# A mirrored, paired layout of attention factors: two long runs for one matmul, two runs for another

## The chip, the cores and the metric

The kernel runs on one core of a Trainium2 chip. The metric is the device time of one execution in microseconds (us), as the median of several runs; less is better. The inputs are 16 graphs of 1024 nodes with 256 features, in fp32, and a 1024 x 1024 int32 adjacency matrix for each.

## The reference, cut to what matters

Each graph goes through two layers, each followed by a residual and a layer norm. The first weighs neighbours by a sigmoid of a leaky-ReLU score. The second is a graph attention layer with 4 heads of 64 features:

```
Wh    = (X @ W).reshape(B, N, H, F)
e     = leaky_relu(e_src[:, :, None, :] + e_dst[:, None, :, :], 0.2)
e     = where(A > 0, e, -1e9)
alpha = softmax(e, axis=2)
Hout  = elu(einsum('bijh,bjhf->bihf', alpha, Wh))
```

The exponential of a leaky ReLU of a sum is exp(s+d) where s+d >= 0 and exp(0.2(s+d)) elsewhere; both split into a factor of the row i and a factor of the column j. So the layer needs, for each row and head, the sum of exp(d_j) Wh_j over the edges with s+d >= 0, and the sum of exp(0.2 d_j) Wh_j over the other edges. The kernel gets the latter as the sum over all edges less the sum over the positive ones.

## The kernel before, in words

Every graph is worked in blocks of 128 nodes (P = 128; NB = 8 blocks; NH = 2 halves of 512 rows; H = 4 heads; F = 64; E = 2F + 2 = 130 columns of factors for each head; F1 = F + 2 = 66).

- **Factors.** `exps` (L598 to L601, ScalarE) makes es[1] = exp(d), es[0] = exp(0.2 d) and rho = exp(-0.8 s). `product` (L619, VectorE) multiplies them into Wh, head by head. `high` (L633, ScalarE) rounds each product to fp32r into the tile `gm`, and `low` (L640, VectorE) puts the remainder of the rounding beside it. `gm` is one tile for the whole run, shaped [128, head, block, level, 130]: level 0 the rounded part, level 1 the remainder. The 130 columns are 64 of exp(d) Wh, 64 of exp(0.2 d) Wh, and the two exponentials.
- **Sums over positive edges.** `pos` (L658, VectorE) makes for a half, a head and a block the 0/1 matrix of positive edges [128 x 512]. `acc` (L670, TensorE) takes it in four slices of 128 as weights, and streams the two levels of one head and block, 260 columns in a row. There are 256 such matmuls for a graph. `acc_low` (L685, ScalarE) copies the low half out of PSUM and `acc_sum` (L693, VectorE) adds the halves into the tile `u`.
- **Sums over all edges.** `all_edges` (L705) casts the mask to fp32r; `total` (L713, TensorE) streams, for each block and level, the columns 64 to 130 of all four heads: four runs of 66 columns, 264 in all. There are 128 such matmuls for a graph. `total_kept` (L749) and `total_less` (L755) take the result out of PSUM.
- **The end of a graph.** `weigh` (L772, L780), `divide` (L790 to L795), `elu` (L816) and `join` (L807, L810) combine the parts in `u`, and the norm follows. In the last graph the fourth head of the second half has steps of its own (`weigh_end` L826, `divide_end` L837 to L848, `elu_end` L855, `join_end` L865, L867). The last two graphs scale on ScalarE (L767) in the function `times`.
- **The other TensorE work** is the score matmuls of the first layer (L356), its aggregation (L427), the projection (L517) and transposes (L319, L395, L498).

The order of all work on every engine is written out by hand: each step of each stage has a due time in a table (TIMES for the middle graphs, FIRST and LAST for the first and the last), a graph's times are shifted by PERIOD = 112, and `issue` calls the steps in the order of these times. So the stages of two or three graphs are interleaved. Semaphore waits follow from which tiles, or which parts of a tile, an instruction touches.

Of the kernel before, what the change touches and what calls it, by code (L numbers as in the profile page):

```python
# [8 lines left out]
F32 = mybir.dt.float32  # L9
F32R = mybir.dt.float32r  # L10
# [3 lines left out]
I32 = mybir.dt.int32  # L14
AF = mybir.ActivationFunctionType
ALU = mybir.AluOpType
# [3 lines left out]
SLOPE = 0.2  # L20
# [7 lines left out]
P = 128  # L28
HALF = 512
# [164 lines left out]
def stages(nc, k, pl, b, xg, adjg, outg, sums, span, zinv):  # L194


    H, F, D, N, NB, DC, NH = k.H, k.F, k.D, k.N, k.NB, k.DC, k.NH
    F1, WD, E = k.F1, k.WD, k.E
    NQ = NB // NH
    HEADS = [(half, h) for half in range(NH) for h in range(H)]  # L200

    TOTALS = [*range(NQ, NB), *range(NQ)]

    first, last, late = b == 0, b == k.B - 1, b >= k.B - 2
    t = {}

    def bank(name):
# [5 lines left out]
    def small(name, *shape, bufs=None):  # L213
        return pl.small.tile([P, *shape], F32, tag=name, name=name, bufs=bufs)
# [43 lines left out]
    def aload():  # L258
        for ib in range(NB):
            if first and 2 <= ib < 6:  # L260

                tile = pl.us.tile([P, 2, H, E], F32, tag="us", name="a_us")
                tile = tile.rearrange("p q h e -> p (q h e)")[:, 0:N].bitcast(I32)
            else:
                tile = pl.adjp.tile([P, N], I32, tag="a32", name="a32")
            t["a32", ib] = tile
            nc.sync.dma_start(out=t["a32", ib], in_=adjg[ib * P : (ib + 1) * P, :])
            yield
# [325 lines left out]
        yield  # L594

    def exps():
        es = t["es"] = small("es", 2, NB, H)
        nc.scalar.activation(es[:, 1], t["cm"], AF.Exp)  # L598
        nc.scalar.activation(es[:, 0], t["cm"], AF.Exp, scale=SLOPE)
        t["rho"] = small("rho", NB, H)  # L600
        nc.scalar.activation(t["rho"], t["sd"], AF.Exp, scale=SLOPE - 1.0)  # L601
        yield


    FACTORS = [(h, s) for h in range(H) for s in range(2)]

    def product():
        for h, s in FACTORS:
# [15 lines left out]

    def factor(h, s):
        if s == 0:
            yield slice(2 * F, E), t["es"][:, :, :, h].rearrange("p s b -> p b s")
        yield slice(s * F, (s + 1) * F), t["prod", h, s]

    def high():  # L630
        for h, s in FACTORS:
            for cols, val in factor(h, s):
                nc.scalar.copy(pl.gm[:, h, :, 0, cols], val)  # L633
            yield

    def low():
        for h, s in FACTORS:
            for cols, val in factor(h, s):
                hi = pl.gm[:, h, :, 0, cols].bitcast(F32)
                nc.vector.tensor_tensor(pl.gm[:, h, :, 1, cols], val, hi, ALU.subtract)  # L640
            yield


# [20 lines left out]
    def acc():  # L664
        for half, h in HEADS:
            for pair in range(NQ // 2):
                t["acc", half, h, pair] = pl.ps_u.tile([P, 2, HALF], F32, tag="u", name="acc")
            for jb in range(NB):
                for q in range(NQ):
                    nc.tensor.matmul(  # L670
                        t["acc", half, h, q // 2][:, q % 2, 0 : 2 * E],
                        lhsT=t["pos", half, h, jb][:, q * P : (q + 1) * P],
                        rhs=pl.gm[:, h, jb].rearrange("p l f -> p (l f)"),
                        start=(jb == 0),
                        stop=(jb == NB - 1),
                    )
                yield
# [10 lines left out]
    def acc_sum():  # L688
        for half, h in HEADS:
            for pair in range(NQ // 2):  # L690
                if h == 0:
                    t["u", half, pair] = pl.us.tile([P, 2, H, E], F32, tag="us", name="u")
                nc.vector.tensor_tensor(  # L693
                    t["u", half, pair][:, :, h, :],
                    t["acc", half, h, pair][:, :, 0:E],
                    t["low", half, h, pair], ALU.add,
                )
                yield


    def all_edges():
# [6 lines left out]
    def total():  # L708
        for ib in TOTALS:
            tot = t["tot", ib] = bank("tot")  # L710
            for jb in range(NB):
                for l in range(2):
                    nc.tensor.matmul(  # L713
                        tot[:, 0 : H * F1],
                        lhsT=t["allm", ib, jb // 4 * 4][:, jb % 4, :],
                        rhs=pl.gm[:, :, jb, l, F:E],
                        start=(jb == 0 and l == 0),
                        stop=(jb == NB - 1 and l == 1),
                    )
                if jb % 2:  # L720
                    yield

    def heads_of(tot):
        return tot[:, 0 : H * F1].rearrange("p (h f) -> p h f", h=H)

    def heads(half):

        return slice(0, H - 1 if last and half else H)

    def parts(half, pair, hs):  # L730

        u = t["u", half, pair][:, :, hs]
        return u[..., 0:F], u[..., F : 2 * F], u[..., 2 * F], u[..., 2 * F + 1]

    def second(half, pair):

        return t["u", half, pair][..., F : 2 * F + 1]

    def nodes(half, pair):
        return t["y", half][:, 2 * pair : 2 * pair + 2, :].rearrange(  # L740
            "p q (h f) -> p q h f", h=H
        )

    def total_kept():
        for ib in TOTALS[:NQ]:
            pair, q = divmod(ib - NQ, 2)
            if q == 0:
                t["ts", pair] = pl.ts.tile([P, 2, H, F1], F32, tag="ts", name="ts")
            nc.scalar.copy(t["ts", pair][:, q], heads_of(t["tot", ib]))  # L749
            yield  # L750

    def total_less():
        for ib in TOTALS[NQ:]:
            u = second(0, ib // 2)[:, ib % 2]
            nc.vector.tensor_tensor(u, heads_of(t["tot", ib])[..., 0 : F + 1], u, ALU.subtract)  # L755
            yield

    PAIRS = [(half, pair) for half in range(NH) for pair in range(NQ // 2)]  # L760

    def times(val, by):

        if late:
            for q in range(2):
                for h in range(val.shape[2]):
                    nc.scalar.activation(  # L767
                        val[:, q, h, :], val[:, q, h, :], AF.Copy, scale=by[:, q, h : h + 1]
                    )
        else:  # L770
            by = by.unsqueeze(3).to_broadcast(list(val.shape))
            nc.vector.tensor_tensor(val, val, by, ALU.mult)  # L772

    def weigh():
        for half, pair in PAIRS:
            ib, hs = half * NQ + 2 * pair, heads(half)
            u2 = second(half, pair)[:, :, hs]
            if half:
                ts = t["ts", pair][:, :, hs, 0 : F + 1]
                nc.vector.tensor_tensor(u2, ts, u2, ALU.subtract)  # L780
                yield
            times(u2, t["rho"][:, ib : ib + 2, hs])
            yield

    def divide():
        t["rz"] = small("rzs", NB, H)
        for half, pair in PAIRS:
            ib, hs = half * NQ + 2 * pair, heads(half)
            o, u2, z2, z1 = parts(half, pair, hs)
            nc.vector.tensor_tensor(o, o, u2, ALU.add)  # L790
            yield
            rz = t["rz"][:, ib : ib + 2, hs]
            nc.vector.scalar_tensor_tensor(rz, z1, Z_MIN, z2, ALU.max, ALU.add)
            yield
            nc.vector.reciprocal(rz, rz)  # L795
            yield
            times(o, rz)
            yield


    def join():
        for half, pair in PAIRS:
            o, ex, _, _ = parts(half, pair, heads(half))
            yp = nodes(half, pair)[:, :, heads(half)]
            rows = (0, 1) if last and half else (slice(0, 2),)
            for q in rows:
                nc.vector.scalar_tensor_tensor(o[:, q], o[:, q], 0.0, yp[:, q], ALU.max, ALU.add)  # L807
            yield
            for q in rows:
                nc.vector.scalar_tensor_tensor(yp[:, q], ex[:, q], 1.0, o[:, q], ALU.min, ALU.add)  # L810
            yield
# [10 lines left out]
    def weigh_end():  # L822
        for h, pair in END:
            if last:
                u2 = second(1, pair)[:, :, h]
                nc.vector.tensor_tensor(u2, t["ts", pair][:, :, h, 0 : F + 1], u2, ALU.subtract)  # L826
            yield

    def divide_end():
# [529 lines left out]
def gnn_resnorm_kernel(  # L1359
# [14 lines left out]
    nc = tc.nc  # L1374
    const = ctx.enter_context(tc.tile_pool(name="const", bufs=1))
    B, N, D = x.shape
    H = a_src.shape[0]
# [10 lines left out]
    with ExitStack() as fast:  # L1388
# [11 lines left out]
        with tc.tile_pool(name="first", bufs=1) as first:  # L1400
            make_constants(nc, k, const, first)
        pl.fill()
        pl.gm = pl.big.tile([P, H, NB, 2, k.E], F32R, tag="gm", name="gm")
        with tc.manual_schedule():
            issue(graphs)
        bad = pl.small.tile([P, 4], F32, tag="bad", name="bad", bufs=1)
# [71 lines left out]
```

## Time and profile before

| what | us |
|---|---|
| median of 3 runs (lowest, highest) | 1742.5 (1742.15, 1743.12) |
| span of the profiled execution | 1739.6 |
| what lies around that span, by the median of the runs | 2.9 |
| TensorE matmul busy | 1692.1 (97%) |
| VectorE busy | 1639.6 (94%) |
| ScalarE busy | 1239.4 (71%) |
| GpSimd busy | 106.8 (6%) |

The time of the profiled execution is not given beside its span, so the span stands for it and the 2.9 us are carried over from the runs. Busy time of TensorE counts a matmul from its first column to its drained result, so neighbours overlap: an `acc` matmul lasts 283 ns, but the next one starts far earlier. The chain view cuts that overlap: it follows the work that ended last back in time, and gives for each piece only the time that it added.

### The profile page before, as it was taken

The page shows a single profiled execution, that of the slowest core. Times are in us where ns is not written, and L with a number is a line of the kernel's source. Part 1 is how long each engine was busy: PE and PEld are TensorE (multiplying, and loading weights), DVE is VectorE, ACT ScalarE, POOL GpSimd, SP SyncE. Part 2 cuts the span into 40 slices and gives each one's busy share as a digit, 9 for nine tenths or more (in the row PEclk, how much of TensorE's full clock was granted, in tenths as well). Part 3 has the DMA queues.
Part 4 walks back from the last instruction along what each step waited for, and adds up shares of the span by engine and source line. Part 5 has one row for each costly group of instructions (what it writes and reads, how often), then busy time and mean ns, then how long its engine had stood idle before and what let it go on. Part 6 is the DMA issues. An engine that isn't in the chain of part 4 may idle for free.

```text
span 1739.6 us, 29647 instructions
## 1 busy us (share of the span) xinstructions
PE 1692.1 (97%) x10580; PEld 1492.5 (86%) x10580; DVE 1639.6 (94%) x3663; ACT 1239.4 (71%) x2766; POOL 106.8 (6%) x138
## 2 busy tenths in 40 slices
PE   8999999999999999999999999999999999999984
PEld 5789898998979889898998979889898898979883
DVE  5498999999999999999999999999999999999998
ACT  7674957759587685967759587685967859586784
POOL 0000000010000101000010000101000010000100
PEclk9999999999999999999999999999999999999987
DMA  5542333434334343333435334443343424422020
GB/s 190 129 116 67 98 98 92 110 92 131 88 89 101 105 125 92 94 101 92 109 92 129 91 86 102 105 128 91 89 107 92 110 67 117 105 71 55 26 68 26
DMA packets 249005, 168.59 MB, mean 97 GB/s; under 512 B 133010, under 2 KB 232468, under 8 KB 248852
## 3 DMA queue, kind: packets, MB, share of 16 engines
q1 hardware_dynamic: 248848, 166.63, 36.1%
q8 instruction: 86, 1.41, 0.3%
q14 instruction: 67, 0.55, 0.1%
q10 hardware_dynamic: 4, 0.00, 0.0%
HBM read 118.10 MB, written 17.04 MB: 78 GB/s over the span
## 4 chain that ended last, share of the span: by engine, by line
PE 91%; DVE 3%; ACT 2%; DMA 1%; issue 1%; POOL 0%; SPq 0%; ACTq 0%; DVEq 0%; POOLq 0%
PE acc L670 27%; PE agg L427 24%; PE tot L713 14%; PE e L356 13%; PE pw L517 7%; PE pg L395 3%; PE pt L498 2%; PE pt L319 1%; DVE pos L658 1%; DMA sbc<-sdram 1%; ACT prod L614 0%; DMA aT<-a 0%; PE pbc L591 0%; ACT gm L633 0%; ACT y L489 0%
## 5 line engine op out<-in xcount | busy, mean ns | idle before, releaser
L658 DVE SCALAR_TENSOR_TENSOR pos<-sbc,nd,mT 128x512 fp32r<-128x512 f32 x1024 | 737.4, 745 | 10.5 <-PE acc L670 5.0
L670 PE MATMUL acc<-gm,pos 128*128 128x260 f32 x4096 | 608.6, 292 | 8.9 <-DVE gm L640 5.0
L670 PEld LDWEIGHTS acc<-gm,pos 128*128 128x128 f32 x4096 | 536.8, 190 | 19.8 <-issue 5.7
L427 PE MATMUL agg<-xb,gate 128*128 128x256 f32 x2048 | 463.5, 379 | 0.2
L427 PEld LDWEIGHTS agg<-xb,gate 128*128 128x128 f32 x2048 | 379.9, 190 | 47.6 <-DVE gate L419 1.2
L713 PE MATMUL tot<-gm,allm 128*128 128x264 f32 x2048 | 328.8, 297 | 5.4 <-ACT gm L633 4.9
L713 PEld LDWEIGHTS tot<-gm,allm 128*128 128x128 f32 x2048 | 281.4, 189 | 9.7 <-ACT gm L633 5.1
L356 PE MATMUL e<-xT,xTa 128*128 128x512 f32 (+3 forms) x768 | 264.3, 489 | 2.2 <-ACT xTa L344 1.4
L356 PEld LDWEIGHTS e<-xT,xTa 128*128 128x128 f32 x768 | 135.1, 191 | 106.4 <-issue 55.3
L685 ACT COPY low<-acc 128x260 f32<-128x260 f32 x256 | 89.8, 377 | 187.5 <-PE acc L670 187.3
L705 ACT CAST allm<-mT 128x512 fp32r<-128x512 uint8 x256 | 157.4, 615 | 33.4 <-PE tot L713 31.7
L489 ACT ACTIVATE y<-y,shift,rstd 128x256 f32<-128x256 f32 x254 | 136.3, 592 | 48.6 <-DVE shift L477 48.6
L276 ACT ACTIVATE a<-a 128x1024 bf16<-128x1024 int32 x124 | 131.3, 1059 | 32.1 <-DMA aT<-a 23.0
L298 ACT ACTIVATE mT<-aT 128x1024 uint8<-128x1024 bf16 x120 | 127.1, 1059 | 7.6 <-DMA aT<-a 7.5
L468 POOL TENSOR_SCALAR std<-mv 128x4 f32<-128x4 f32 x64 | 27.7, 432 | 1618.7 <-DVE mv L450 1447.1
L517 PE MATMUL pw<-w_aug,yT 128*128 128x264 f32 x512 | 121.8, 387 | 0.5 <-ACT yT L507 0.5
L376 DVE TENSOR_TENSOR gate<-e,gate 128x512 f32<-128x512 f32 x192 | 105.5, 556 | 14.5 <-ACT gate L368 14.4
L693 DVE TENSOR_TENSOR u<-acc,low 128x260 f32<-128x260 f32 x256 | 103.1, 425 | 10.5 <-ACT low L685 10.3
L444 DVE BATCH_NORM_STATS2 st<-y 128x6 f32<-128x256 f32 x256 | 107.5, 421 | 1.2
L517 PEld LDWEIGHTS pw<-w_aug,yT 128*128 128x128 f32 x512 | 93.4, 190 | 15.4 <-ACT yT L507 1.9
L368 ACT ACTIVATE gate<-e 128x512 f32<-128x512 f32 x192 | 90.2, 486 | 13.7 <-PE e L356 13.3
L412 DVE TENSOR_TENSOR gate<-gate,mT 128x1024 f32<-128x1024 f32 (+7 forms) x128 | 96.6, 755 | 2.9 <-ACT mT L298 2.4
(111 smaller groups left out, 1788.8 us busy)
## 6 DMA issues: line engine op xcount, KB each, us to landing
a<-in_adj_dram SPq DMA_DIRECT2D x124, 512.0 KB, 4.6
sbc<-sdram SPq DMA_DIRECT2D x128, 256.0 KB, 4.6
out_dram<-y SPq DMA_DIRECT2D x31, 512.0 KB, 3.5
xb<-in_x_dram SPq DMA_DIRECT2D x15, 1024.0 KB, 5.4
a_us<-in_adj_dram SPq DMA_DIRECT2D x4, 512.0 KB, 8.9
aT<-a SPq DMA_TRANSPOSE x120, 3.1
xb<-in_x_dram SPq DMA_DIRECT2D x2, 512.0 KB, 4.7
sdram<-srow SPq DMA_DIRECT2D x32, 8.0 KB, 1.4
```

The costliest lines, as they stand in the source:

```text
L276: nc.scalar.activation(t["a16", ib], t["a32", ib], AF.Copy, accum_out=sums[:, 0, at : at + 1])
L298: nc.scalar.activation(t["mT"][:, :, ib * P : (ib + 1) * P], t["aT", ib], AF.Square, accum_out=sums[:, 1, at : at + 1],)
L356: nc.tensor.matmul(e[:, 0:n], lhsT=t["xTa", jb][:, c, :], rhs=t["xT"][:, c, at : at + n], start=(c == 0), stop=(c == DC - 1),)
L376: nc.vector.tensor_tensor(ge, t["e", jb, at][:, 0:n], ge, ALU.max)
L427: nc.tensor.matmul(agg[:, 0:D], lhsT=t["gate"][:, jb, ib * P : (ib + 1) * P], rhs=t["xb"][:, jb, :], start=(jb == 0), stop=(jb == NB - 1),)
L444: nc.vector.bn_stats(st, t["y", half][:, q, :])
L489: nc.scalar.activation(y, y, AF.Identity, bias=shift, scale=rstd)
L517: nc.tensor.matmul(pw[:, 0:WD], lhsT=t["yT"][:, c, jb * P : (jb + 1) * P], rhs=k.w_aug[:, c, :], start=(c == 0), stop=(c == DC - 1),)
L658: nc.vector.scalar_tensor_tensor(p_, t["sbc", half, h], t["nd"][:, jb, h : h + 1], t["mT"][:, jb, half * HALF : (half + 1) * HALF], ALU.is ...
L670: nc.tensor.matmul(t["acc", half, h, q // 2][:, q % 2, 0 : 2 * E], lhsT=t["pos", half, h, jb][:, q * P : (q + 1) * P], rhs=pl.gm[:, h, jb] ...
L705: nc.scalar.copy(m_, t["mT"][:, j0 : j0 + 4, ib * P : (ib + 1) * P])
L713: nc.tensor.matmul(tot[:, 0 : H * F1], lhsT=t["allm", ib, jb // 4 * 4][:, jb % 4, :], rhs=pl.gm[:, :, jb, l, F:E], start=(jb == 0 and l == 0),
```

## The change

Heads are grouped in pairs (0, 1) and (2, 3), in all graphs but the last, which keeps the old layout (`last`).

- `gm` becomes [128, pair, block, level, 2 x 130]. The even head of a pair has its columns as before (first factor, second factor, exp(0.2 d), exp(d)); the odd head has them mirrored (exp(d), exp(0.2 d), second factor, first factor). So the 66 + 66 columns that the sum over all edges needs lie next to each other.
- `total` streams two runs of 132 columns, not four of 66.
- `acc` streams, for a head, two runs of 130 columns that lie 260 apart, not one run of 260. Its output in PSUM stays 260 columns in a row. An odd head's runs start 520 bytes into the pair's row.
- `exps` computes exp(0.2 d) once more (es[2]), so that an odd head finds its two columns beside each other in mirrored order.
- `acc_sum` adds 2 x 66 columns for each of two row blocks (264 elements, not 260), so that `u` gets slots of 132 columns; the two spare columns of an odd head fall on places that the even head then overwrites. For that the heads go in the order 1, 0, 3, 2.
- The steps after it read `u` through strided views: 4 (row block and pair) x 2 (head) x 64 or 65.
- `u` is a flat tile of 1056 columns; the last graph takes its old shape from a slice of it (`whole`).
- The tables of due times are not touched.

```
-    HEADS = [(half, h) for half in range(NH) for h in range(H)]
+    ORDER = [*range(H)] if last else [h ^ 1 for h in range(H)]
+    HEADS = [(half, h) for half in range(NH) for h in ORDER]
...
-        es = t["es"] = small("es", 2, NB, H)
+        es = t["es"] = small("es", 3, NB, H)
         nc.scalar.activation(es[:, 1], t["cm"], AF.Exp)
-        nc.scalar.activation(es[:, 0], t["cm"], AF.Exp, scale=SLOPE)
+        for s in (0, 2)[: 1 if last else 2]:
+            nc.scalar.activation(es[:, s], t["cm"], AF.Exp, scale=SLOPE)
...
+    AT = [(0, F, 2 * F), (0, F, 2 * F) if last else (F + 2, 2, 0)] * (H // 2)
+    def gm_of(h):
+        if last:
+            return pl.gm.rearrange("p (h b l e) -> p h b l e", h=H, l=2, e=E)[:, h]
+        pairs = pl.gm.rearrange("p (g b l i e) -> p g i b l e", g=H // 2, l=2, i=2, e=E)
+        return pairs[:, h // 2, h % 2]
+    def gm_second(jb, l):
+        if last:
+            gm = pl.gm.rearrange("p (h b l e) -> p h b l e", h=H, l=2, e=E)
+            return gm[:, :, jb, l, F:E]
+        pairs = pl.gm.rearrange("p (g b l e) -> p g b l e", g=H // 2, l=2, e=2 * E)
+        return pairs[:, :, jb, l, F : F + 2 * F1]
...
                     nc.tensor.matmul(
-                        t["acc", half, h, q // 2][:, q % 2, 0 : 2 * E],
+                        t["acc", half, h, q // 2][:, q % 2, 0 : 2 * E].rearrange(
+                            "p (l e) -> p l e", l=2
+                        ),
                         lhsT=t["pos", half, h, jb][:, q * P : (q + 1) * P],
-                        rhs=pl.gm[:, h, jb].rearrange("p l f -> p (l f)"),
+                        rhs=gm_of(h)[:, jb],
...
-                nc.vector.tensor_tensor(
-                    t["u", half, pair][:, :, h, :],
-                    t["acc", half, h, pair][:, :, 0:E],
-                    t["low", half, h, pair], ALU.add,
-                )
+                if last:
+                    u = whole(half, pair)[:, :, h, :]
+                    nc.vector.tensor_tensor(u, acc[:, :, 0:E], low, ALU.add)
+                else:
+                    at = h // 2 * 2 * (E + 2)
+                    at, step = (at + E + F1, -F1) if h % 2 else (at, F1)
+                    nc.vector.tensor_tensor(
+                        view(t["u", half, pair][:, :], at, [H * (E + 2), 2], [step, 2], [1, F1]),
+                        view(acc[:, :, :], 0, [HALF, 2], [F, 2], [1, F1]),
+                        view(low[:, :, :], 0, [E, 2], [F, 2], [1, F1]), ALU.add,
+                    )
...
+    def view(a, at, *steps):
+        return bass.AP(a.tensor, a.offset + at, [a.ap[0], *steps])
+    def whole(half, pair):
+        u = t["u", half, pair][:, 0 : 2 * H * E]
+        return u.rearrange("p (q h e) -> p q h e", q=2, h=H)
...
-                        tot[:, 0 : H * F1],
+                        by_pair(tot[:, 0 : H * F1]),
                         lhsT=t["allm", ib, jb // 4 * 4][:, jb % 4, :],
-                        rhs=pl.gm[:, :, jb, l, F:E],
+                        rhs=gm_second(jb, l),
...
+    def by_pair(tot):
+        return tot if last else tot.rearrange("p (g f) -> p g f", g=H // 2)
     def heads_of(tot):
-        return tot[:, 0 : H * F1].rearrange("p (h f) -> p h f", h=H)
+        if last:
+            return tot[:, 0 : H * F1].rearrange("p (h f) -> p h f", h=H)[..., 0 : F + 1]
+        n = tot.shape[1] // (2 * F1)
+        return view(tot, 0, [2 * F1, n], [F + 3, 2], [1, F + 1])
...
+    def spaced(half, pair, at, step, *last):
+        return view(t["u", half, pair][:, :], at, [2 * (E + 2), H], [step, 2], *last)
     def second(half, pair):
-        return t["u", half, pair][..., F : 2 * F + 1]
+        if last:
+            return whole(half, pair)[..., F : 2 * F + 1]
+        return spaced(half, pair, F1, E + 1, [1, F + 1])
...
-        pl.gm = pl.big.tile([P, H, NB, 2, k.E], F32R, tag="gm", name="gm")
+        pl.gm = pl.big.tile([P, H * NB * 2 * k.E], F32R, tag="gm", name="gm")
```

More of the change, by code (lines that the diff above doesn't have):

```diff
@@ L199, in stages @@
     NQ = NB // NH
-    HEADS = [(half, h) for half in range(NH) for h in range(H)]
+    first, last, late = b == 0, b == k.B - 1, b >= k.B - 2
+    ORDER = [*range(H)] if last else [h ^ 1 for h in range(H)]
+    HEADS = [(half, h) for half in range(NH) for h in ORDER]
     TOTALS = [*range(NQ, NB), *range(NQ)]
-    first, last, late = b == 0, b == k.B - 1, b >= k.B - 2
     t = {}
@@ L260, in aload @@
             if first and 2 <= ib < 6:
-                tile = pl.us.tile([P, 2, H, E], F32, tag="us", name="a_us")
-                tile = tile.rearrange("p q h e -> p (q h e)")[:, 0:N].bitcast(I32)
+                tile = pl.us.tile([P, 2 * H * (E + 2)], F32, tag="us", name="a_us")
+                tile = tile[:, 0:N].bitcast(I32)
             else:
@@ L602, in exps @@
         yield
-    FACTORS = [(h, s) for h in range(H) for s in range(2)]
+    FACTORS = [(h, s) for h in ORDER for s in range(2)]
+    AT = [(0, F, 2 * F), (0, F, 2 * F) if last else (F + 2, 2, 0)] * (H // 2)
[10 more added lines that the diff above has]
+        return pairs[:, :, jb, l, F : F + 2 * F1]
     def product():
@@ L626, in factor @@
         if s == 0:
-            yield slice(2 * F, E), t["es"][:, :, :, h].rearrange("p s b -> p b s")
-        yield slice(s * F, (s + 1) * F), t["prod", h, s]
+            at, odd = AT[h][2], h % 2 and not last
+            yield slice(at, at + 2), t["es"][:, odd : odd + 2, :, h].rearrange("p s b -> p b s")
+        yield slice(AT[h][s], AT[h][s] + F), t["prod", h, s]
     def high():
@@ L632, in high @@
             for cols, val in factor(h, s):
-                nc.scalar.copy(pl.gm[:, h, :, 0, cols], val)
+                nc.scalar.copy(gm_of(h)[:, :, 0, cols], val)
             yield
@@ L638, in low @@
             for cols, val in factor(h, s):
-                hi = pl.gm[:, h, :, 0, cols].bitcast(F32)
-                nc.vector.tensor_tensor(pl.gm[:, h, :, 1, cols], val, hi, ALU.subtract)
+                hi = gm_of(h)[:, :, 0, cols].bitcast(F32)
+                nc.vector.tensor_tensor(gm_of(h)[:, :, 1, cols], val, hi, ALU.subtract)
             yield
@@ L690, in acc_sum @@
             for pair in range(NQ // 2):
-                if h == 0:
-                    t["u", half, pair] = pl.us.tile([P, 2, H, E], F32, tag="us", name="u")
-                nc.vector.tensor_tensor(
-                    t["u", half, pair][:, :, h, :],
-                    t["acc", half, h, pair][:, :, 0:E],
-                    t["low", half, h, pair], ALU.add,
-                )
-                yield
+                if h == ORDER[0]:
+                    t["u", half, pair] = pl.us.tile(
+                        [P, 2 * H * (E + 2)], F32, tag="us", name="u"
+                    )
+                acc, low = t["acc", half, h, pair], t["low", half, h, pair]
+                if last:
[8 more added lines that the diff above has]
+                        view(low[:, :, :], 0, [E, 2], [F, 2], [1, F1]), ALU.add,
+                    )
+                yield
+    def view(a, at, *steps):
[3 more added lines that the diff above has]
+        return u.rearrange("p (q h e) -> p q h e", q=2, h=H)
     def all_edges():
@@ L721, in total, with rows_of @@
                     yield
+    def by_pair(tot):
+        return tot if last else tot.rearrange("p (g f) -> p g f", g=H // 2)
     def heads_of(tot):
-        return tot[:, 0 : H * F1].rearrange("p (h f) -> p h f", h=H)
+        if last:
+            return tot[:, 0 : H * F1].rearrange("p (h f) -> p h f", h=H)[..., 0 : F + 1]
+        n = tot.shape[1] // (2 * F1)
+        return view(tot, 0, [2 * F1, n], [F + 3, 2], [1, F + 1])
     def heads(half):
         return slice(0, H - 1 if last and half else H)
-    def parts(half, pair, hs):
-        u = t["u", half, pair][:, :, hs]
-        return u[..., 0:F], u[..., F : 2 * F], u[..., 2 * F], u[..., 2 * F + 1]
+    def rows_of(a):
+        if last:
+            return a
+        if len(a.shape) == 4:
+            return a.rearrange("p q (g i) f -> p (q g) i f", i=2)
+        return a.rearrange("p q (g i) -> p (q g) i", i=2)
+    def spaced(half, pair, at, step, *last):
+        return view(t["u", half, pair][:, :], at, [2 * (E + 2), H], [step, 2], *last)
+    def parts(half, pair, hs):
+        if last:
+            u = whole(half, pair)[:, :, hs]
+            return u[..., 0:F], u[..., F : 2 * F], u[..., 2 * F], u[..., 2 * F + 1]
+        o, u2 = (spaced(half, pair, at, E + 2, [1, F]) for at in (0, F1))
+        return o, u2, spaced(half, pair, E, F1 + 1), spaced(half, pair, E + 1, F + 1)
     def second(half, pair):
-        return t["u", half, pair][..., F : 2 * F + 1]
+        if last:
+            return whole(half, pair)[..., F : 2 * F + 1]
+        return spaced(half, pair, F1, E + 1, [1, F + 1])
     def nodes(half, pair):
@@ L747, in total_kept @@
             if q == 0:
-                t["ts", pair] = pl.ts.tile([P, 2, H, F1], F32, tag="ts", name="ts")
-            nc.scalar.copy(t["ts", pair][:, q], heads_of(t["tot", ib]))
+                t["ts", pair] = pl.ts.tile([P, 2, H * F1], F32, tag="ts", name="ts")
+            nc.scalar.copy(t["ts", pair][:, q], t["tot", ib][:, 0 : H * F1])
             yield
@@ L753, in total_less, with kept @@
         for ib in TOTALS[NQ:]:
-            u = second(0, ib // 2)[:, ib % 2]
-            nc.vector.tensor_tensor(u, heads_of(t["tot", ib])[..., 0 : F + 1], u, ALU.subtract)
+            u = second(0, ib // 2)
+            u = u[:, ib % 2] if last else u[:, ib % 2 * H // 2 :][:, 0 : H // 2]
+            tot = heads_of(t["tot", ib][:, 0 : H * F1])
+            nc.vector.tensor_tensor(u, tot, u, ALU.subtract)
             yield
+    def kept(pair):
+        ts = t["ts", pair]
+        if last:
+            ts = ts.rearrange("p q (h f) -> p q h f", h=H)
+            return ts[..., 0 : F + 1]
+        return heads_of(ts.rearrange("p q e -> p (q e)"))
     PAIRS = [(half, pair) for half in range(NH) for pair in range(NQ // 2)]
@@ L764, in times @@
         if late:
-            for q in range(2):
+            for q in range(val.shape[1]):
                 for h in range(val.shape[2]):
@@ L776, in weigh @@
             ib, hs = half * NQ + 2 * pair, heads(half)
-            u2 = second(half, pair)[:, :, hs]
+            u2 = second(half, pair)
+            u2 = u2[:, :, hs] if last else u2
             if half:
-                ts = t["ts", pair][:, :, hs, 0 : F + 1]
+                ts = kept(pair)[:, :, hs] if last else kept(pair)
                 nc.vector.tensor_tensor(u2, ts, u2, ALU.subtract)
                 yield
-            times(u2, t["rho"][:, ib : ib + 2, hs])
+            times(u2, rows_of(t["rho"][:, ib : ib + 2, hs]))
             yield
@@ L791, in divide @@
             yield
-            rz = t["rz"][:, ib : ib + 2, hs]
+            rz = rows_of(t["rz"][:, ib : ib + 2, hs])
             nc.vector.scalar_tensor_tensor(rz, z1, Z_MIN, z2, ALU.max, ALU.add)
@@ L803, in join @@
             o, ex, _, _ = parts(half, pair, heads(half))
-            yp = nodes(half, pair)[:, :, heads(half)]
-            rows = (0, 1) if last and half else (slice(0, 2),)
+            yp = rows_of(nodes(half, pair)[:, :, heads(half)])
+            rows = (0, 1) if last and half else (slice(None),)
             for q in rows:
@@ L825, in weigh_end @@
                 u2 = second(1, pair)[:, :, h]
-                nc.vector.tensor_tensor(u2, t["ts", pair][:, :, h, 0 : F + 1], u2, ALU.subtract)
+                nc.vector.tensor_tensor(u2, kept(pair)[:, :, h], u2, ALU.subtract)
             yield
```

## The prediction

> **What bounds the kernel now.** First I read the page's busy times and clock, then the table of stages, to see whether TensorE only looks full.
>
> ```profile
> PE 1692.1 (97%) x10580; PEld 1492.5 (86%) x10580; DVE 1639.6 (94%) x3663; ACT 1239.4 (71%) x2766; POOL 106.8 (6%) x138
> ...
> PEclk9999999999999999999999999999999999999987
> ...
> 224.00:1568.00 1344.00, 1343.37 (x8430) 1188.99 (x8430) 1313.28 (x2912) 973.80 (x2114) 86.80 (x104) 1.00 0.38 100
> 1709.00:1740.00 31.00, 8.67 (x59) 7.70 (x57) 22.63 (x83) 14.32 (x47) 2.64 (x4) 0.67 0.11 36
> ```
>
> In the middle 1344 us TensorE (first busy column) is idle for 0.6 us at the full granted clock (1.00); VectorE (third) is idle for 30.7 us, ScalarE for 370. A graph starts every 104.56 us there (the chain shows the same piece of 24 score matmuls at 396.19 and, eleven graphs on, at 1546.38), so VectorE has 2.4 us of idle time for each graph. A busy TensorE need not stream, so I take the pitch of matmuls (what each adds) from the chain of work, in a stretch where it is all TensorE:
>
> ```profile
> 1683.51 1.50 PE tot L713 x12
> 1685.01 2.40 PE acc L670 x20
> ...
> 1690.36 2.54 PE tot L713 x20
> 1692.89 1.44 PE acc L670 x12
> ...
> 1697.74 1.00 PE tot L713 x8
> ```
>
> Columns: start, us, work. Acc: 2.40/20 = 1.44/12 = 120 ns for 260 columns in one run. Tot: 1.50/12 = 125, 2.54/20 = 127, 1.00/8 = 125 ns for 264 columns in four runs. Over all neighbours in the trace that end under 160 ns apart, the means are 119.9 (acc) and 125.5 (tot). With the pitches of the other matmuls, read in the same way (aggregation 216 ns, chain piece of 24 in 5.18 us; scores 429 to 111; projection 223; transposes 109), a graph adds up to 256 x 119.9 + 128 x 125.5 + 57.3 = 104.05 us of streaming: 99.5% of its 104.56. So a nanosecond on a matmul is a nanosecond on the time, and work for VectorE or ScalarE is free until VectorE's 2.4 us per graph are gone.
>
> The last view is the end, where TensorE is out of work and VectorE and ScalarE hand the last graph to each other:
>
> ```profile
> 1723.36 0.53 ACT L816 ACTIVATE u<-u 128x384 f32<-128x384 f32 x1
> ...
> 1723.79 0.40 DVE L848 TENSOR_SCALAR u<-u,rzs 128x64 f32<-128x64 f32 x2
> ...
> 1724.23 0.31 ACT L855 ACTIVATE u<-u 128x128 f32<-128x128 f32 x1 [0.34 <-DVE u L848]
> 1724.27 0.59 DVE L807 SCALAR_TENSOR_TENSOR u<-u,y 128x192 f32<-128x192 f32 x2
> ...
> 1724.44 1.53 ACT L767 ACTIVATE u<-u,rzs 128x64 f32<-128x64 f32 x6
> ...
> 1726.00 0.52 ACT L816 ACTIVATE u<-u 128x384 f32<-128x384 f32 x1
> ...
> 1726.31 0.42 DVE L848 TENSOR_SCALAR u<-u,rzs 128x64 f32<-128x64 f32 x2
> ```
>
> **The change part by part.** Fifteen graphs change layout: 15 x 256 = 3840 acc and 15 x 128 = 1920 tot matmuls. In the order of the changed program, the position of every instruction and the waits of these fifteen graphs are as before, except for 15 more exponentials; new waits stand only at the end of the last graph.
>
> *Price of a run.* Acc's pitch scaled to 264 columns is 119.9 x 264/260 = 121.8 ns. Tot stands 3.7 ns above that, with three more breaks: 1.2 ns a break, if each costs the same. Then tot goes from four runs to two: 2 x 1.2 x 1920 = 4.7 us less. Acc goes from one to two: 1.2 x 3840 = 4.7 us more. It cancels for any price, since the runs streamed in a graph are the same in number: 256 + 128 x 4 = 768 before, 256 x 2 + 128 x 2 = 768 after. Net 0.
>
> *Alignment.* Tot's level 0 runs start on a multiple of 16 bytes and its level 1 runs 8 bytes off. Their mean pitches are 124.5 and 126.3 ns. After, tot's runs are all aligned, and the odd heads' two acc runs are 8 bytes off. Per run: 960 x 4 such runs before, 1920 x 2 after, net 0. Per matmul: 1.8 x (1920 - 960) = 1.7 us more. I take 0.
>
> *Bounds of these.* Low: only short runs pay, and runs of 130 pay nothing: 3.7 x 1920 = 7.1 us less. High: the first break pays all: 3.7 x 3840 = 14.2 us more, and tot keeps its pitch. Larger `u` and `es` tiles also move addresses; single acc places (block and slice) have means from 117.4 to 122.3 ns, so the mean could shift by 1 ns either way: 5.8 us over all 5760. I take 0, as nothing gives this a sign.
>
> [...]
>
> *VectorE.* Sixteen acc_sum per graph add 264 elements, not 260: at (697 - 425)/260 = 1.05 ns an element (L772's 520 against L693's 260) 4.2 ns each, 1.0 us over 240. Hidden in the 2.4 us per graph; 1.0 if that cover were gone. The strided steps keep their element counts; four runs of 65 (L755, 418 ns) against two of 130 (L693, 425 ns) show that runs cost nothing there. Half of the 65-column runs now start on an odd word, which no row of before shows.
>
> [...]
>
> *ScalarE.* Fifteen exponentials of 32 columns at 213 ns (the row of L599) are 3.2 us, in 370 us of idle time. Behind each wait rho and the first copies into `gm`; TensorE's idle time on those is 0.0 in the middle, so I take 0. In the first graph up to 0.2 may show. Upper bound 3.2.
>
> *The end.* The old `u` was a four-dimensional tile; the last graph now cuts its shape from a flat one, and the changed order has waits that come of overlap in range, not in elements. The scaling at L848 waits for the exponential L816 of the other heads, and the exponential L855 waits for both join rows at L807. From the rows: the first L848 moves from 1723.79 to L816's end, 1723.89. L855 must wait for L807's end, 1724.27 + 0.59 = 1724.86, plus 0.1 of signalling: 0.7 late. Behind it on ScalarE stand the six scalings and the second L816, which then ends at 1726.52 + 0.7 = 1727.2. The second L848, at 1726.31 before, waits for that: 1727.3, 1.0 late, and behind it on VectorE stand the last joins, moments and the norm. With 0.1 for the first pair: 1.1 us. Bounds 0.3 (slack that I don't see) and 1.8 (both waits in full).
>
> *Sum.* 0 (runs) + 0 (VectorE) + 0.1 (ScalarE, first graph) + 1.1 (end) = 1.2 us, on the span of 1739.6: 1740.8. The median of the runs stands 2.9 above that span: 1743.7.
>
> **The rivals.**
>
> *A, forecast: runs cancel.* For it: the two pitches fit one price per run. 1743.7.
>
> *B, faster: only short runs pay.* At TensorE's rate a break could hide behind a long run. Against it: acc's own pitch changes with its address (117.4 to 122.3 ns), so that long runs aren't free of what reading costs. 1742.5 - 7.1 + 1.2 = 1736.6; with half the effect 1740.2.
>
> *C, slower: a broken pattern pays once, whatever the number of runs.* For it: 1.2 ns a break was only argued from the end point of three. Against: nothing in this trace has exactly two runs. 1742.5 + 14.2 + 1.2 = 1757.9; with half 1750.8. It decides from 2.3 us beyond the end's 1.2 on, that is where acc's 3840 matmuls cost 0.6 ns each more than tot gives back.
>
> *D, slower: VectorE becomes the bound.* Some 46 of its instructions per graph get new views. If each were 52 ns longer, 2.4 us would be used up; at 70 ns the overrun is 0.8 us per graph, 12 us in all: 1756. Against: the equal rows for 65 and 130.
>
> *E, the change does not do what it says.* In the changed program the moving patterns are 2 x 132 and 2 x 130 in fifteen graphs, so I give this nothing.
>
> **How the numbers follow.** About 0.2% (3.5 us) is what a measurement of this kernel can tell from no change. A 0.56 with B 0.15, C 0.22 (half or full), D 0.07. Within 0.2% falls most of A (0.45) and the weaker ends of B and C (0.05): 0.50. Faster: B's rest 0.12 and 0.02 of A by addresses: 0.14. Slower: C and D without their weak ends, and 0.09 of A by alignment and addresses: 0.36. The range reaches to B in full (1736.6) and past half of C (1750.8): 1737 to 1752, with 0.07 left below and 0.12 above. The likeliest case's own range is 1738 to 1749.
>
> **What would show it.** Right: tot's pitch in the chain falls to about 123 ns, acc's rises to about 121, the stretch 224 to 1568 holds the same graphs within 2 us, acc_sum takes some 4 ns more, and the second L848's successor starts about 1 us later against the last acc. Wrong: acc at 122.5 or more with tot still at 125 (C), tot at 122 with acc at 120 (B), or TensorE idle before acc with VectorE as releaser in the middle (D).

## The result and the profile after

The changed kernel takes 1745.4 us (median of 21 runs), the kernel before 1742.9 us (21 runs). The ratio is 1.0014, with a 95% interval of 1.0008 to 1.0021: 1.4 to 3.7 us slower. The difference of the medians, 2.5 us or 0.14%, lies inside the 0.2% that the prediction called no change, on the slower side; the interval's end just reaches it. The forecast was 1743.7 us.

The page of the changed kernel, its busy times and the three groups that the change touches (line, engine, operation, shapes, count; busy us and mean ns of one; idle time before them):

```profile
PE 1694.1 (97%) x10580; PEld 1494.0 (86%) x10580; DVE 1640.6 (94%) x3663; ACT 1241.4 (71%) x2781; POOL 106.8 (6%) x138
...
L692 PE MATMUL acc<-gm,pos 128*128 128x260 f32 x4096 | 615.0, 294 | 9.6 <-DVE gm L662 5.0
...
L754 PE MATMUL tot<-gm,allm 128*128 128x264 f32 x2048 | 324.2, 295 | 5.4 <-ACT gm L655 4.9
...
L727 DVE TENSOR_TENSOR u<-acc,low 128x264 f32<-128x264 f32 x240 | 96.9, 425 | 10.2 <-ACT low L709 10.1
```

The same three groups before:

```profile
L670 PE MATMUL acc<-gm,pos 128*128 128x260 f32 x4096 | 608.6, 292 | 8.9 <-DVE gm L640 5.0 <-DVE u L693 3.8 <-DVE pos L658 0.2
...
L713 PE MATMUL tot<-gm,allm 128*128 128x264 f32 x2048 | 328.8, 297 | 5.4 <-ACT gm L633 4.9 <-DVE gm L640 0.4
...
L693 DVE TENSOR_TENSOR u<-acc,low 128x260 f32<-128x260 f32 x256 | 103.1, 425 | 10.5 <-ACT low L685 10.3
```

Acc's busy time has gained 6.4 us and tot's has lost 4.6. The 15 new exponentials are in ScalarE's count (2781, from 2766). The sums into `u` (L727) add 264 elements and still take 425 ns, as with 260.

The same stretch of the middle as before, in the table of stages (length, then busy time of TensorE, weight load, VectorE, ScalarE, GpSimd, with counts; granted clock, DMA share, GB/s):

```profile
224.00:1568.00 1344.00, 1343.41 (x8418) 1188.39 (x8417) 1312.35 (x2908) 973.85 (x2124) 86.76 (x104) 1.00 0.39 100
```

TensorE is idle for 0.6 us, as before, and VectorE for 31.7 us (30.7 before). Together with the graphs below this says that the bound hasn't moved: TensorE streams nearly without a gap at a granted clock of 1.00, and VectorE still has idle time.

In the chain of work, the pieces of one graph of the changed kernel (start, us, work):

```profile
352.90 0.98 PE tot L754 x8
353.87 1.94 PE acc L692 x16
...
361.30 5.18 PE agg L430 x24
366.48 2.92 PE acc L692 x24
```

and the same four pieces of the kernel before:

```profile
352.71 1.00 PE tot L713 x8
353.71 1.91 PE acc L670 x16
...
361.14 5.18 PE agg L427 x24
366.32 2.87 PE acc L670 x24
```

Here lies what changes in a graph: 24 acc matmuls take 2.92 us, not 2.87, eight tot matmuls take 0.98, not 1.00, and the 24 aggregations, which the change doesn't touch, take 5.18 in both. (The pieces that the prediction showed, at 1683 us and after, belong to the last graph, which keeps its layout; so they could not show a change.)

A piece of the chain is rounded to 10 ns, so I add up whole graphs: for the six undisturbed graphs of a trace (those with the shortest distance from the first acc of one graph to the first acc of the next), the time from each matmul's start to the next one's, by what the matmul is.

| us per graph | acc (256) | tot (128) | all other | sum |
|---|---|---|---|---|
| before | 32.93 | 17.19 | 54.32 | 104.44 |
| after | 33.41 | 16.87 | 54.28 | 104.56 |

So acc costs 0.48 us more (1.9 ns a matmul) and tot gives back 0.32 us (2.5 ns a matmul); 0.12 us per graph are left, 1.8 us in 15 graphs. Mean pitches of neighbouring matmuls of one kind (ends under 160 ns apart, as in the prediction, over the 15 graphs that change) say the same: acc 119.9 to 121.6 ns, tot 125.6 to 122.7.

The rest is at the end. The timeline of the changed kernel there (start, us, engine, line, operation, tiles; in brackets the idle time before it and what ended it):

```profile
1716.26 4.53 PE L692 MATMUL acc<-gm,pos 128*128 128x260 f32 x32 [0.69 <-DVE u L722]
...
1726.16 0.52 ACT L890 ACTIVATE u<-u 128x384 f32<-128x384 f32 x1
...
1726.71 0.42 DVE L922 TENSOR_SCALAR u<-u,rzs 128x64 f32<-128x64 f32 x2
...
1727.21 0.58 DVE L881 SCALAR_TENSOR_TENSOR u<-u,y 128x192 f32<-128x192 f32 x2
...
1727.89 0.31 ACT L929 ACTIVATE u<-u 128x128 f32<-128x128 f32 x1 [1.21 <-DVE u L911]
1728.11 1.53 ACT L840 ACTIVATE u<-u,rzs 128x64 f32<-128x64 f32 x6
...
1729.66 0.52 ACT L890 ACTIVATE u<-u 128x384 f32<-128x384 f32 x1
1730.22 0.42 DVE L922 TENSOR_SCALAR u<-u,rzs 128x64 f32<-128x64 f32 x2 [0.82 <-ACT u L890]
```

These are the rows L816, L848, L807, L855, L767 of before with new numbers. L929 sits idle for 1.21 us until both join rows at L881 are done (1727.21 + 0.58 = 1727.79), and the second L922 sits idle for 0.82 us until the exponential L890 is done. Neither wait was there before. (The bracket of L929 names L911, a short step that follows L881 on VectorE and ended at 1727.86; the changed program's wait is for the second L881.) The stretch from the start of the last acc row to VectorE's last comparison is read from the chain of work, before

```profile
1713.46 4.31 PE acc L670 x30
...
1733.97 0.14 DVE flag L1427
```

and after (the acc row starts at 1716.26, above):

```profile
1737.94 0.14 DVE flag L1501
```

It was 20.51 us and is now 21.68 us: 1.17 us more.

1.8 us from the matmuls and 1.2 us from the end make 3.0 us, within the interval of 1.4 to 3.7. The two profiled executions lie further apart, 4.1 us (1739.6 and 1743.7). About 1 us of that stands in the last graph ahead of its last acc row (59.8 us from its first acc to there, 58.8 before); the kernels below that move the factor tile by 8 bytes or keep acc in one run show 60.2 and 60.0 us there without the flat tile in that graph, so I don't count it to the change.

### The profile page after: what moved, and what is told of

It is laid out like the page before. It is cut to its first block, busy times and chain, and to the rows that moved or that the text cites. A ratio compares the mean times of both kernels' runs of the same rounds, so it can differ in the third digit from the quotient of the medians.

```text
span 1743.7 us, 29670 instructions
## 1 busy us (share of the span) xinstructions
PE 1694.1 (97%) x10580; PEld 1494.0 (86%) x10580; DVE 1640.6 (94%) x3663; ACT 1241.4 (71%) x2781; POOL 106.8 (6%) x138
## 4 chain that ended last, share of the span: by engine, by line
PE 86%; DVE 3%; issue 3%; ACT 3%; DMA 2%; POOL 0%; SPq 0%; DVEq 0%; POOLq 0%; ACTq 0%
PE acc L692 26%; PE agg L430 23%; PE tot L754 13%; PE e L359 12%; PE pw L520 7%; PE pg L398 2%; PE pt L501 2%; PE pt L322 1%; DVE pos L680 1%; DMA sbc<-sdram 1%; ACT prod L635 0%; ACT gm L655 0%; ACT mT L301 0%; ACT y L492 0%; DMA aT<-a 0%
## 5 line engine op out<-in xcount | busy, mean ns | idle before, releaser
L692 PE MATMUL acc<-gm,pos 128*128 128x260 f32 x4096 | 615.0, 294 | 9.6 <-DVE gm L662 5.0
L754 PE MATMUL tot<-gm,allm 128*128 128x264 f32 x2048 | 324.2, 295 | 5.4 <-ACT gm L655 4.9
L301 ACT ACTIVATE mT<-aT 128x1024 uint8<-128x1024 bf16 x120 | 127.0, 1059 | 8.2 <-DMA aT<-a 8.2
L727 DVE TENSOR_TENSOR u<-acc,low 128x264 f32<-128x264 f32 x240 | 96.9, 425 | 10.2 <-ACT low L709 10.1
```

The lines of the kernel that those rows point to most:

```text
L301: nc.scalar.activation(t["mT"][:, :, ib * P : (ib + 1) * P], t["aT", ib], AF.Square, accum_out=sums[:, 1, at : at + 1],)
L692: nc.tensor.matmul(t["acc", half, h, q // 2][:, q % 2, 0 : 2 * E].rearrange("p (l e) -> p l e", l=2), lhsT=t["pos", half, h, jb][:, q * P ...
L754: nc.tensor.matmul(by_pair(tot[:, 0 : H * F1]), lhsT=t["allm", ib, jb // 4 * 4][:, jb % 4, :], rhs=gm_second(jb, l), start=(jb == 0 and l ...
```

## The experiments

My theory going in was the prediction's: each break in the moving columns (the columns of `gm` that a matmul streams) costs 1.2 ns, so the runs cancel, and the end is 1.1 us later by the waits of the flat tile. The rival to the first half was a price by lines: what counts is how many lines of 16 bytes, counted from the tile's start, the columns touch (acc 65 before and 66 after, tot 68 and 66). It fits the pitches of before: 125.5/119.9 = 1.047, and 68/65 = 1.046. Both give a sum near 0 for the change itself (by lines 256 x 1 - 128 x 2 = 0 a graph), so the change itself can't tell them apart. Four kernels, after the first one here, can.

**The end alone.** The changed kernel, in which only the last graph's `u` is a four-dimensional tile again:

```
-                    t["u", half, pair] = pl.us.tile(
-                        [P, 2 * H * (E + 2)], F32, tag="us", name="u"
-                    )
+                    shape = [P, 2, H, E + 2] if last else [P, 2 * H * (E + 2)]
+                    t["u", half, pair] = pl.us.tile(shape, F32, tag="us", name="u")
...
-        u = t["u", half, pair][:, 0 : 2 * H * E]
-        return u.rearrange("p (q h e) -> p q h e", q=2, h=H)
+        return t["u", half, pair][:, :, :, 0:E]
```

> The changed kernel, but the last graph's u is again a tile of four dimensions (slots of 132 columns), so that its waits are those of before; nothing else differs. Theory of the end (the new waits cost 1.1 us there, the changed profile shows 21.68 us from the start of the last acc matmuls' row to the last comparison on VectorE against 20.51): the stretch goes back to 20.5 us and the time falls by 1.2 us, to 1744.2, about 1.3 us above before, which is what the matmul pitches leave (3840 x 1.7 less 1920 x 2.8). Rival (the end moved because of the clock or by chance): the stretch stays at 21.7 and the time at 1745.4.

Measured: ratio 1.0004 (0.9995 to 1.0013), 1743.9 us against 1743.0 of the kernel before on that chip. Its timeline at the end, and the last comparison from its chain:

```profile
1713.59 4.54 PE L692 MATMUL acc<-gm,pos 128*128 128x260 f32 x32 [0.69 <-DVE u L721]
...
1723.92 0.40 DVE L920 TENSOR_SCALAR u<-u,rzs 128x64 f32<-128x64 f32 x2
...
1724.35 0.31 ACT L927 ACTIVATE u<-u 128x128 f32<-128x128 f32 x1 [0.34 <-DVE u L920]
1724.40 0.59 DVE L879 SCALAR_TENSOR_TENSOR u<-u,y 128x192 f32<-128x192 f32 x2
```

```profile
1734.10 0.14 DVE flag L1499
```

The exponential (L927) starts before the join rows (L879), with 0.34 us of idle time ahead of it as in the kernel before, and from the last acc row to the last comparison (1734.10) it is 20.51 us, exactly as before. The graphs are those of the changed kernel: acc 33.41, tot 16.87, sum 104.55. So the end's 1.17 us belong to the shape of that one tile. The time has an interval too wide to show 1.2 us by itself; the trace shows it.

**One run, moved by 8 bytes.** The kernel before, with nothing changed but where `gm` begins:

```
-        pl.gm = pl.big.tile([P, H, NB, 2, k.E], F32R, tag="gm", name="gm")
+        pl.gm = pl.big.tile([P, H * NB * 2 * k.E + 2], F32R, tag="gm", name="gm")
+        pl.gm = pl.gm[:, 2:].rearrange("p (h b l e) -> p h b l e", h=H, b=NB, l=2)
```

> The kernel before, with the whole factor tile moved by 8 bytes: acc still streams one run of 260 columns, but from an address 8 bytes off a multiple of 16; tot's levels swap their alignment. Theory of lines (a read costs by the 16-byte lines that it touches): acc goes from 65 lines to 66, its pitch from 119.9 to 121.8 ns, as in the changed kernel; tot stays at 68 lines; 4096 x 1.85 = 7.6 us slower, 1750.5. Theory of runs (each break between runs costs some 1.3 to 1.7 ns, alignment nothing): acc stays at 119.9, the time at 1742.9. Theory of alignment by matmul (1.8 ns for one that starts off 16 bytes, from tot's two levels): 7.4 us slower through acc, and tot's level 0 becomes the slower one.

Measured: ratio 1.0041 (1.0027 to 1.0055), 1749.6 us. Its chain of work, the same pieces as above:

```profile
352.92 1.93 PE acc L670 x16
...
360.34 5.18 PE agg L427 x24
365.52 2.95 PE acc L670 x24
```

Acc still reads one run of 260 columns, and yet costs as much as, or more than, the changed kernel's two runs (2.95 us for 24 against 2.92; 33.46 us per graph). By the count of lines, its 1040 bytes touch 66 lines of 16 bytes from this start, not 65. The price of a break falls here: there is no break, and the price is paid. The third theory of the expectation, a price for a start 8 bytes off, fits this run as well as the lines do: it foretold the same acc, and tot's level 0 did become the slower one (126.3 against 124.7 ns). The next run tells these two apart.

**Acc in two runs, tot as it was.** The kernel before, with the two levels of a head apart (`gm` as [128, head, level, block, 130]):

```
-                        rhs=pl.gm[:, h, jb].rearrange("p l f -> p (l f)"),
+                        rhs=pl.gm[:, h, :, jb],
...
-                        rhs=pl.gm[:, :, jb, l, F:E],
+                        rhs=pl.gm[:, :, l, jb, F:E],
```

> The kernel before, with the two levels of a head's factors in separate halves of its part of the tile: acc streams two runs of 130 columns, tot four of 66 as before. Half of the change alone. If the two prices are independent and cancel in the changed kernel: acc's pitch goes from 119.9 to 121.6 or 121.8 ns, tot stays at 125.5; 4096 x 1.7 to 1.85 = 7.0 to 7.6 us slower, 1750. If acc paid for something else in the changed kernel (moved tiles, paired heads): acc stays at 119.9 and the time at 1742.9.

Measured: ratio 1.0039 (1.0025 to 1.0052), 1750.1 us; acc 33.42 us per graph, tot 17.17.

```profile
354.44 1.96 PE acc L670 x16
...
361.91 5.18 PE agg L427 x24
367.10 2.93 PE acc L670 x24
```

This is acc's half of the change alone, and it is as large as the prediction's cancelling terms said: 0.49 us x 16 = 7.8 us by the graphs, 7.1 us by the times. Both theories said so; the run shows that the changed kernel's small difference is indeed two larger ones.

This run also answers the price for a start 8 bytes off. A block of a level is 520 bytes here, so acc's two runs both start on a multiple of 16 in the even blocks and both 8 bytes off in the odd ones, with 66 lines in either. The mean pitches are 121.9 ns in the even blocks and 121.6 in the odd. Tot's four runs change in the same way, with 68 lines in either: 125.8 and 125.7. At equal lines the start alone costs nothing that shows.

**Tot in two runs for half of its matmuls, acc in one.** A head's 260 columns are one run again, but ordered so that the level 0 columns that tot needs lie beside those of the pair's other head. So tot reads two runs of 132 at level 0, and four of 66 at level 1; the runs of 132 start 8 bytes off, so that they touch 2 x 34 = 68 lines:

```
     def gm_at(h, level, cols):
...
+        if h % 2:
+            at += 2 * E + (level * F1 if at < F1 else F1 + (1 - level) * F)
+        else:
+            at += level * F if at < F else F + (1 - level) * F1
...
+        s0 = 2 * E - F1
+        if l == 0:
+            return pairs[:, :, jb, s0 : s0 + 2 * F1].rearrange("p g (i f) -> p g i f", i=2)
+        a = pairs[:, :, jb, s0 - F1 : s0 - F1 + F1]
+        return bass.AP(a.tensor, a.offset, [*a.ap[:-1], [3 * F1, 2], [1, F1]])
```

(`at` enters as the column in the layout of before, in an odd head in its mirror image.)

> A layout between the two, with the last graph's own tile as in the first run: an even head's 260 columns are first factor level 0, level 1, second factor level 1, level 0, an odd head's the mirror image, and the heads of a pair stand side by side. So acc streams one run of 260 again; tot streams two runs of 132 for level 0 (8 bytes off 16) and four of 66 for level 1. Theory of runs: acc 119.9, tot's level 0 at 122.9 (two breaks fewer), level 1 at 125.5: 960 x 2.6 = 2.5 us faster than before, 1740.4. Theory of lines: acc 65 lines, tot 68 in both levels (two runs of 528 bytes from 8 bytes off touch 34 each): the same as before, 1742.9.

Measured: ratio 1.0005 (0.9996 to 1.0014), 1743.7 us; acc 32.94 us per graph, tot 17.24 (17.19 before).

```profile
352.35 1.01 PE tot L769 x8
353.36 1.92 PE acc L708 x16
...
360.80 5.18 PE agg L430 x24
365.98 2.87 PE acc L708 x24
```

Half of tot's matmuls have two breaks fewer, and the graph wins nothing by it: level 0 has a mean pitch of 125.4 ns, where a price per break would have made it 122.9 and tot's sum 17.02 us. Level 1, with four runs, stands at 126.7 in this kernel; but levels of four runs differ by more among themselves (124.5 and 126.3 in the kernel before), so no price of a break can be read from that. Together with the run moved by 8 bytes, this speaks for lines against breaks: price without a break there, breaks away without a gain here.

One rival is left. In every kernel here a matmul's lines are either all read in full (acc with 65, tot with 66) or some are read by half (acc with 66, tot with 68). So a price that a matmul pays once, when any of its runs begins or ends inside a line, fits as well as a price for each line; a tot with 67 lines would tell them apart, and none was run.

**The control: moved by 16 bytes.** As the second run, with 4 columns in place of 2.

> The kernel before, with the tile gm moved by 16 bytes, not by 8: the control for the run that moved it by 8 bytes. If the price goes by lines of 16 bytes (65 for acc, 68 for tot, as before), acc stays at 119.9 ns and tot at 125.5, and the time is that of the kernel before, 1743 us within 2. If the tile's address in itself, or the changed allocation, made that run slower, this one is slower too: acc near 122 ns and about 1749 us.

Measured: ratio 1.0005 (0.9996 to 1.0014), acc 32.99 us per graph, tot 17.25. Sixteen bytes cost nothing that can be told from no change, 8 bytes cost 0.4%. It is not the move, but where the run starts: by the count of 16-byte lines acc touches 65 here and 66 there. The 0.06 us by which each of acc and tot differs from before (0.2 ns a matmul in acc, 0.5 in tot) is a measure of what an address does besides.

**How much VectorE can take.** That VectorE's work is hidden, and that 2.4 us per graph would have to be used up before it shows, carried three terms and a rival of the prediction. The kernel before, with some of the sums into `u` done a second time, into a tile that nobody reads (4, 8 or all 16 of a graph):

```
                     t["low", half, h, pair], ALU.add,
                 )
+                if pair == 0:
+                    nc.vector.tensor_tensor(
+                        pl.spare, t["acc", half, h, pair][:, :, 0:E],
+                        t["low", half, h, pair], ALU.add,
+                    )
                 yield
```

> The kernel before, with 4 of the 16 acc_sum of each graph done a second time, into a tile that nobody reads: extra work for VectorE of 4 x 0.42 = 1.7 us per graph. VectorE was idle for 2.4 us per graph, so if that idle time can take any work, the time stays at 1743 us, or grows by up to 1.7 us at the two ends. If the idle time is cut into pieces that this work can't use, up to 1.7 x 16 = 27 us show: 1770 us.

> As the run before it, with 8 of 16 acc_sum done twice: 3.4 us per graph against 2.4 us of idle time. If VectorE's idle time is the cover, 1.0 us per graph is left over: 1.0 x 14 graphs = 14 us, with 2 to 3 us more at the ends: about 1759 us, VectorE without idle time in the middle, and TensorE waiting for it there. If TensorE stayed the bound, 1743 to 1746 us. If nothing is covered, 54 us: 1797 us.

> As the run before it, with all 16 acc_sum done twice: 6.8 us per graph against 2.4 us of idle time. If VectorE's idle time is the cover, 4.4 us per graph are left over: 62 us over 14 graphs, with some 6 us at the ends: about 1810 us. If nothing is covered, 109 us: 1852 us. The step from 8 to 16 should then cost all of its 3.4 us per graph, some 50 us.

| sums done twice | ratio (95% interval) | us per graph |
|---|---|---|
| 4 | 1.0012 (1.0003 to 1.0021) | 104.46 |
| 8 | 1.0087 (1.0071 to 1.0102) | 105.19 |
| 16 | 1.0300 (1.0284 to 1.0315) | 107.75 |

The first is free in most graphs (in its profile, three of them were 0.9 to 1.4 us longer, for which I have no cause; the run moved by 16 bytes, without any added work, has three such graphs too, 0.8 to 1.1 us longer, so they need not come of VectorE), the second shows, the third shows in full. But the sizes are smaller than expected: 16 instead of 8 cost 2.57 us per graph, not 3.4, and the whole time grew by 52 us, not 68. VectorE's timeline with 16 says why:

```profile
599.76 0.42 DVE L699 TENSOR_TENSOR spare<-acc,low 128x260 f32<-128x260 f32 x1
600.09 0.42 DVE L444 BATCH_NORM_STATS2 st<-y 128x6 f32<-128x256 f32 x1
```

An instruction shown as 0.42 us is followed by the next one 0.33 us later: neighbours on VectorE overlap. From the end of a sum into `u` to the end of the extra one it is 0.335 us (256 cases). So the added work was 1.34, 2.68 and 5.36 us per graph, and the growth of 0.02, 0.75 and 3.31 us leaves 1.9 and 2.0 us hidden in the last two. The cover is about 2.0 us per graph, somewhat less than the idle time of 2.4.

With 8, the table of stages hardly shows that the bound has changed:

```profile
224.00:1568.00 1344.00, 1342.73 (x8369) 1179.56 (x8368) 1331.12 (x2994) 964.39 (x2092) 106.84 (x104) 1.00 0.38 100
```

TensorE is idle for 1.3 us of 1344, where the graphs are 0.7% longer. The chain of work does show it: it goes through VectorE for long stretches there.

```profile
630.42 0.75 DVE pos L658
631.18 0.34 DVE u L693
631.51 2.65 DVE pos L658 x4
634.16 0.41 DVE u L785
```

Only with 16 do TensorE's waits name VectorE, beside ScalarE (what waited, for what: us, times, longest):

```profile
PE ptop L588 <- ACT xT L330: 2.9, 12, 0.2
PE acc L670 <- DVE spare L699: 2.5, 13, 0.2
PE acc L670 <- DVE rzs L800: 1.7, 9, 0.2
```

## Why the prediction was right, and where it was not

- *TensorE is the bound, a nanosecond on a matmul is one on the time.* Right. The pitches and the graphs changed together: acc and tot changed by +0.48 and -0.32 us per graph, everything else by -0.04, and the graph by 0.12.
- *Price of a run: cancels, net 0.* The cancelling was right, the reason was not. The step put the 3.7 ns of tot over acc down to three more breaks at 1.2 ns. The run moved by 8 bytes has acc dearer with no break more, and the run with tot in two runs of 132 has two breaks fewer at no gain. What the runs agree with is the number of 16-byte lines: acc with 65 lines stood at 119.9 to 120.0 ns in three kernels, with 66 lines at 121.6 to 122.0 in four; tot with 68 lines at 125.3 to 126.1, with 66 at 122.7. Whether the price goes by the number of lines or is paid once for any line read by half stays open. By lines the sum is 0 too, so the prediction's number did not suffer. That is the luck of this layout: acc gains one break and one line, tot loses two of each, so the two rules can't differ in it. As a rule for the next layout, the prediction's step would have been wrong: it promised a gain for the kernel with tot in two runs that is not there (122.9 ns at level 0 by it, 125.4 measured).
- *Its size.* By lines, the sum was one more for 256 matmuls and two fewer for 128: 0. Measured it is 0.12 us per graph, 1.8 us in all, since acc's one line cost 1.9 ns and tot's two gave 2.5 ns, not 3.7. This term, forecast as 0, is about what the change exceeds its forecast by: 2.5 us were measured where 1.2 were forecast. (The time itself lies 1.7 us above the forecast; 0.4 of that is the kernel before, 1742.9 in 21 runs against the 1742.5 in three that the forecast started from.) Why a line is worth less in tot than in acc stays open. The move by 16 bytes shifts either by 0.06 us per graph, so that addresses alone could account for much of the 0.12.
- *Alignment.* I took 0, against 1.7 us if a start 8 bytes off cost 1.8 ns a matmul. In the changed kernel the odd heads' runs of acc start 8 bytes off and cost what the even heads' cost (odd heads 121.4 and 121.7, even heads 121.9 and 121.5 ns): 130 columns touch 33 lines from either start. Acc in two runs with tot as it was shows the same block by block. That tot's two levels differ by 1.8 ns before at equal lines is not explained by lines. In the run moved by 8 bytes they differ the other way round (126.3 and 124.7), which looks like the start; but with acc in two runs both levels start alike and still differ (126.7 and 125.2). It stays open.
- *VectorE: 4.2 ns each, hidden.* Hidden, and not even there: 425 ns for 264 elements as for 260. The 1.05 ns an element was the slope between two different steps, and four elements more of one step don't show it. The strided steps cost nothing either; the three groups with the new views took 692, 694 and 415 ns (697, 700 and 418 before). Runs of 65 columns that start on an odd word, the case that no row of before had, have no price here.
- *ScalarE: 15 exponentials, hidden.* Nothing of them shows in the middle: all matmuls other than acc and tot take 54.28 us per graph, 54.32 before. The 0.1 us for the first graph can't be checked: its first acc starts at 88.4 us before, at 89.0 in the changed kernel, and at 88.1 in the run with the last graph's own tile, which has the same exponentials.
- *The end, 1.1 us.* Right, step by step, counted from the last acc row: the first L848 came 0.1 us later (forecast 0.1), L855 0.9 (forecast 0.7, with 0.1 for the hand-off, which took 0.1 in the changed kernel: the second L881 ended at 1727.79, L929 started at 1727.89), the second L848 1.1 (forecast 1.0), the last comparison 1.17 (forecast 1.1). With the tile's shape put back all of it is gone. This is the term that the diff doesn't show, and that the order of the changed instructions and its waits does.
- *The rivals.* B (only short runs pay) falls: acc's longer runs pay 1.9 ns. C (the first break pays all) falls with acc at 121.6 and tot at 122.7. D (VectorE becomes the bound) happens with 16 sums done twice (3.0% longer), but the change is far from it: it decides from some 2.0 us per graph, that is 43 ns on each of the 46 instructions, and they grew by none.

## What to carry to other kernels

When TensorE streams without a gap, count for each matmul the 16-byte lines that its moving columns touch, by start and length of each run: in these kernels merging runs paid only where it lowered that count (tot from 68 lines to 66: 125.6 to 122.7 ns; two runs at 68 lines: 125.4), and a start 8 bytes off cost where it added to it (acc in one run, from 65 lines to 66: 32.93 to 33.46 us per graph). Before trading one matmul's layout for another's, multiply by how often each is issued; here one line on 256 and two on 128 all but cancel. And when a tile changes shape, look for the waits it makes at places where it holds several owners' work: here a flat tile cost 1.2 us in one graph with no instruction changed.

## What was not expected of the hardware

- Moving one tile by 8 bytes, with no other change, costs 0.41% (1.0027 to 1.0055) of this kernel; moving it by 16 bytes nothing that can be told (1.0005, 0.9996 to 1.0014).
- A break between runs that adds no line costs nothing that shows: tot at 68 lines has 125.4 ns with two runs and 123.8 to 127.0, by level and kernel, with four.
- VectorE's shown durations overlap: 0.42 us shown, 0.335 us from end to end. The idle time is not the whole cover either: about 2.0 of 2.4 us per graph could be filled.
- With 8 sums done twice TensorE lost 0.7% to VectorE, with 1.3 us of idle time in 1344 to show for it; its busy time covers short waits (an acc matmul is shown as 292 ns where the next starts 120 ns after it). The distance between graphs and the chain show what the busy column doesn't.
